# Two 64-column products or one 128-column product for each step that brings coefficients into place

## The chip, the cores and the metric

The kernel runs on one core of a Trainium2 chip. A core has TensorE (matmuls; PE in the profile, its weight loads PEld), VectorE (DVE), ScalarE (ACT), GpSimd (POOL), and queues that start transfers between HBM and the on-chip memory. A matmul holds one operand, the weights (`lhsT`), in its 128 x 128 array and streams the other (`rhs`) past it; the result goes to PSUM. The metric is the time of one launch on the device in microseconds.

## The reference

Two layers of the same kind act on `x` of shape (2, 56, 128, 128): two images, 56 channels, 128 x 128 points. Each layer is a Fourier attention block with a residual around it:

```python
xn = inorm(xa, g1, b1)                      # xa: every channel by itself
k, q, v = (fno_layer(xn, w) for w in (K, Q, V))   # 1 channel -> 8 heads
attn = softmax(q . k / 128, axis=-1)        # 56 x 56, for each head
out = fno_layer(attn . v, P)                # 8 heads -> 1 channel
att = inorm(out + xa)
h = fno_layer(inorm(att), M0, norm=True, act=gelu)
h = fno_layer(h, M1, norm=True)
x = x + inorm(h) + att                      # with group norm on the input
```

`fno_layer` takes the 2-D Fourier transform, multiplies 32 x 16 low modes by complex coefficients (`Kw`, `Qw`, `Vw`, `Pw`, `M0w`, `M1w`), transforms back and adds a 1 x 1 product of the input. All of it is float32.

## The kernel before

The kernel never builds `k`, `q` and `v` in space. It works on the modes: `modes_chain` brings each image's channels into 32 x 16 modes, `gram`, `scores` and `softmax_chain` form the attention, `values`, `mix_chain` and `heads` apply it, `norms_chain` and `h_chain` work out the norms and the two small layers, `gelu` and `end` come back to space in eight pieces an image. The products with coefficients need these as small matrices, so `prepare` (lines 361 to 466), once a layer, multiplies the raw coefficients (`stage`) to the combinations that are needed (`cpt`), brings them into place with `relay`, and spreads them out into `WU`, `WT` and `WM` with `build` and a last loop.

`relay` (lines 468 to 489) is called three times a layer, with n = 16, 16 and 4 coefficient rows. It transposes `cpt` (8 n rows come out), lays the result out in `L` with four VectorE multiplications by a mask (`m8`), so that each of 8 steps t and two halves e has 64 columns, and then has TensorE multiply these by another mask (`m16`, n columns). That is one unit of 16 products: for each t, e = 0 goes to PSUM partitions 0 to 63 and e = 1 to partitions 64 to 127, given by `tile_position`. One copy brings the 8 n columns from PSUM to `tcs` (tile `tc` in the profile), from where `build` and `WM` take them. `L` lies in `WT` for the first call and in `stage` for the others, so in the profile the products are `psum<-C,WT` with 64 weight columns and `psum<-C,stage`.

The order is written out by hand. Each operation, or group of operations in `with work.unit()`, is a unit; the long string `ORDER` says in which order the units are issued and on which engine, and `PLACES` says which banks of PSUM each takes. `Work.issue` (line 209) makes all calls, so nearly every instruction has the line L215. An engine does its instructions in the order in which they were issued, each when the semaphores that it waits for are there. The work of a `relay` stands in TensorE's queue between work of `turned`, `gram`, `modes_chain`, `scores` and, for the second layer, of `h_chain` and `end` of the layer before.

Names in the profile's steps: `mv` are the sums from which `modes_chain` takes mean and variance, a product with `group` (128 columns); `fwg` is the transform's matrix scaled by that; `sq` is a sum in `h_chain`, a product with `fold` (64 columns); `spread` (line 559, `psum<-C,f` there) lays a column of `f` out over partitions; `inverse` (line 522) ends in VectorE transposes into `WT`.

## Time and profile before

| | |
|---|---|
| median of 3 runs | 369.89 us (367.32 to 373.07) |
| profiled execution, its own time | 372.52 us |
| its span, first to last instruction | 370.7 us |
| mean granted TensorE clock | 0.957 |
| busy: TensorE, its weight loads, VectorE, ScalarE, GpSimd | 329.5, 240.7, 266.2, 232.3, 240.8 us |
| matmuls and weight loads | 7362 of each |

A row of the timeline has the start, the duration, the engine, the code line, the operation, the tiles (out <- in), the shapes and the count; in brackets stands the idle time of the engine before it and what ended it. For a matmul the first shape is that of the weights (rows x columns), the second that of what streams. Rows that follow one another in the same group are merged, and a matmul's end is modelled, so what counts on TensorE is when things start. "issue" is idle time that ends with nothing the profile shows. In the chain of waits a row has start, duration and whose work it is. In the table by windows the last three columns are the granted clock of TensorE, the DMA share and GB/s.

### The profile page before, as it was taken

To read this page: it belongs to the slowest core of one execution; us is meant where nothing else is said; L and a number is where in the kernel's file an instruction comes from. 1 tells how busy PE (TensorE), PEld (TensorE's weight loads), DVE (VectorE), ACT (ScalarE), POOL (GpSimd) and SP (SyncE) were. 2 spreads that over 40 slices of the span, in tenths; PEclk is the share of its full clock that TensorE was granted. 3 is DMA by queue.
4 is the path that set the end of the run, shared out by engine and by line. 5 is a ranking of instruction groups with operands and counts; after the bars stand their busy time and mean duration, and the time that the engine had idled before them with its cause. 6 is when DMAs were issued, how large, how long until landed. Compare 5 with 4: busy or idle time off the path is not lost.

```text
span 370.7 us, 16358 instructions
## 1 busy us (share of the span) xinstructions
PE 329.5 (89%) x7362; PEld 240.7 (65%) x7362; DVE 266.2 (72%) x515; ACT 232.3 (63%) x338; POOL 240.8 (65%) x224
## 2 busy tenths in 40 slices
PE   2549989999999999998979999899999999999970
PEld 1445975888776656567866987698676546665540
DVE  4866963546868876787678956456698877989980
ACT  0437954454456978788883986544476878888400
POOL 7540489719987893278579797716965381467970
PEclk9999998999999999898868999999999999999995
DMA  7998223000053535201512076500045454202886
GB/s 211 273 257 247 63 58 107 4 4 5 2 137 71 156 104 137 52 2 54 177 51 71 10 222 188 147 5 4 2 126 135 129 165 103 52 4 78 252 260 206
DMA packets 15973, 40.14 MB, mean 108 GB/s; under 512 B 2560, under 2 KB 2816, under 8 KB 15904
## 3 DMA queue, kind: packets, MB, share of 16 engines
q1 hardware_dynamic: 12692, 30.84, 30.1%
q10 hardware_dynamic: 3212, 8.27, 7.6%
q8 instruction: 57, 0.93, 1.1%
q14 instruction: 12, 0.10, 0.1%
HBM read 24.42 MB, written 14.68 MB: 105 GB/s over the span
## 4 chain that ended last, share of the span: by engine, by line
PE 54%; DVE 18%; POOL 8%; issue 7%; DMA 6%; ACT 4%; DVEq 0%; ACTq 0%; POOLq 0%
PE psum L215 54%; DVE P L215 7%; DMA X<-x 6%; POOL X L215 4%; DVE X L215 3%; DVE WU L215 3%; DVE WT L215 2%; ACT P L215 2%; DVE psum L215 1%; POOL P L215 1%; POOL der L215 1%; DVE f L215 1%; POOL WT L215 1%; POOL WM L215 1%; ACT WU L215 1%
## 5 line engine op out<-in xcount | busy, mean ns | idle before, releaser
L215 POOL TENSOR_TENSOR X<-X,gvr 128x1024 f32<-128x1024 f32 x29 | 68.5, 2372 | 3.8 <-DMA store<-X 3.7
L215 ACT ACTIVATE junk<-P 128x1024 uint8<-128x1024 f32 (+1 forms) x56 | 56.6, 1011 | 2.1 <-DVE X L215 1.3
L215 PE MATMUL psum<-P 128*56 128x56 f32 (+2 forms) x1664 | 56.5, 224 | 0.0
L215 PEld LDWEIGHTS psum<-C,P 32*128 32x128 f32 (+4 forms) x1124 | 41.5, 159 | 22.1 <-ACT P L215 5.4
L215 PEld LDWEIGHTS psum<-P 128*56 128x56 f32 (+1 forms) x1664 | 50.0, 134 | 4.1 <-ACT P L215 1.1
L215 PE MATMUL psum<-C,P 32*128 32x128 f32 (+4 forms) x1124 | 49.5, 253 | 3.1 <-DVE P L215 1.0
L215 ACT COPY P<-psum 128x896 f32<-128x896 f32 (+3 forms) x30 | 26.9, 916 | 24.3 <-PE psum L215 24.2
L215 POOL TENSOR_TENSOR P<-P,X 128x1024 f32<-128x1024 f32 x14 | 32.8, 2370 | 10.7 <-ACT P L215 10.7
L215 ACT ACTIVATE P<-psum,cols 128x1024 f32<-128x1024 f32 x32 | 34.6, 1115 | 7.5 <-PE psum L215 7.2
L215 PE MATMUL psum<-C,X 56*128 56x56 f32 x512 | 26.1, 263 | 13.2 <-DMA C<-const_all 7.0
L215 ACT ACTIVATE P<-psum 128x896 f32<-128x896 f32 (+1 forms) x28 | 23.9, 857 | 20.4 <-PE psum L215 16.2
L215 PE MATMUL psum<-X,BTx 57*64 57x512 f32 x256 | 35.2, 631 | 0.8 <-ACT WT L215 0.7
L215 PEld LDWEIGHTS psum<-C,X 56*128 56x128 f32 x512 | 23.1, 172 | 17.1 <-DMA X<-x 7.3
L215 DVE SCALAR_TENSOR_TENSOR X<-psum,cols,xr 128x1024 f32<-128x1024 f32 x22 | 27.6, 1272 | 7.3 <-ACT xf L215 3.2
L215 ACT ACTIVATE P<-P,shz,gv 128x1792 f32<-128x1792 f32 x14 | 25.6, 1875 | 11.0 <-PE psum L215 10.6
L215 POOL TENSOR_TENSOR X<-P,X 128x1024 f32<-128x1024 f32 x12 | 28.3, 2378 | 3.7 <-DVE P L215 3.7
L215 DVE STREAM_TRANSPOSE P<-psum 128x448 f32<-128x448 f32 (+1 forms) x24 | 23.6, 1012 | 8.9 <-PE psum L215 8.9
L215 DVE COPY P<-psum 128x896 f32<-128x896 f32 (+4 forms) x27 | 20.4, 766 | 12.7 <-PE psum L215 12.4
L215 POOL TENSOR_TENSOR X<-X,xr 128x1024 f32<-128x1024 f32 x9 | 21.3, 2370 | 10.2 <-ACT X L215 10.2
L215 PE MATMUL psum<-C,WT 32*128 32x128 f32 (+1 forms) x544 | 23.4, 295 | 1.8 <-DVE P L215 1.3
L215 PEld LDWEIGHTS psum<-C,WT 32*128 32x128 f32 (+1 forms) x544 | 19.8, 196 | 8.0 <-DVE P L215 4.6
L215 DVE SCALAR_TENSOR_TENSOR P<-P,hs,psum 128x1024 f32<-128x1024 f32 x17 | 21.2, 1269 | 3.5 <-PE psum L215 3.5
(210 smaller groups left out, 649.7 us busy)
## 6 DMA issues: line engine op xcount, KB each, us to landing
xr<-x SPq DMA_DIRECT2D x30, 224.0 KB
store<-X SPq DMA_DIRECT2D x29, 224.0 KB
xr<-store SPq DMA_DIRECT2D x27, 224.0 KB
out<-P SPq DMA_DIRECT2D x23, 224.0 KB
X<-x SPq DMA_DIRECT2D x9, 448.0 KB
X<-x ACTq DMA_DIRECT2D x7, 448.0 KB
out<-P ACTq DMA_DIRECT2D x9, 224.0 KB
xr<-store ACTq DMA_DIRECT2D x5, 224.0 KB
```

The source lines that it names most:

```text
L215: getattr(engines[letter], method)(*args, **kw)
```

## The change

Each `relay` issues 8 products in place of 16. The weights of a step t are all 128 columns (e, c, j, s in one), the output is all 128 partitions, and no `tile_position` is given. What streams is the same, as are the unit's place in `ORDER`, its bank, and the copy behind it.

```diff
         with work.unit():
             for t in range(8):
-                for e in range(2):
-                    T.matmul(
-                        pt[64 * e : 64 * e + 64, n * t : n * t + n], lhsT=L[:rows, t, e].rearrange("p c j s -> p (c j s)"),
-                        rhs=C["m16"][:rows, :n], start=True, stop=True, tile_position=(0, 64 * e), skip_group_check=True,
-                    )
+                T.matmul(
+                    pt[:, n * t : n * t + n], lhsT=L[:rows, t].rearrange("p e c j s -> p (e c j s)"),
+                    rhs=C["m16"][:rows, :n], start=True, stop=True, skip_group_check=True,
+                )
         copy("SV", tcs[:, :, o : o + n], pt[:, : 8 * n].rearrange("p (t n) -> p t n", t=8))
```

## The prediction

> **What bounds the kernel now.** I read the page first, for the engine that the end hangs on, then the chain of waits around the places where the changed products run, then the timeline of TensorE there.

> ```profile
> span 370.7 us, 16358 instructions
> PE 329.5 (89%) x7362; PEld 240.7 (65%) x7362; DVE 266.2 (72%) x515; ACT 232.3 (63%) x338; POOL 240.8 (65%) x224
> PEclk9999998999999999898868999999999999999995
> PE 54%; DVE 18%; POOL 8%; issue 7%; DMA 6%; ACT 4%; DVEq 0%; ACTq 0%; POOLq 0%
> ```

> TensorE holds 54% of the chain that ends last, three times as much as the next engine. The changed edit touches TensorE alone, so the first question is what it does to TensorE's time, and the second which of the places lies on that chain. The six units that change (three calls of `relay` per layer) are these rows of TensorE's timeline, in order of time:

> ```profile
> 41.28 1.06 PE L215 MATMUL psum<-C,WT 128*64 128x16 f32 x32
> 45.09 1.11 PE L215 MATMUL psum<-C,stage 128*64 128x16 f32 x32
> 53.24 1.05 PE L215 MATMUL psum<-C,stage 32*64 32x4 f32 x30
> 183.85 1.89 PE L215 MATMUL psum<-C,stage 128*64 128x16 f32 x32
> 192.12 1.17 PE L215 MATMUL psum<-C,stage 128*64 128x16 f32 x32
> 222.04 1.10 PE L215 MATMUL psum<-C,stage 32*64 32x4 f32 x32
> ```

> I call them U1 to U6. Each has 32 records for 16 products, so one float32 product is two passes, and each pass has its own weight load. (U3 begins with two more records at 53.11, hence x30.) The chain of waits around them:

> ```profile
> 33.93 11.25 PE psum L215 x346
> 45.20 1.02 ACT P L215 x2
> ...
> 50.67 2.26 PE psum L215 x62
> 52.95 0.17 DVE gs L215
> ...
> 187.56 3.17 PE psum L215 x20
> 190.76 3.29 DVE WT L215 x2
> 194.12 37.18 PE psum L215 x958
> ```

> U1 lies inside the stretch from 33.93, U6 inside that from 194.12. U2 and U3 lie between pieces, U4 before 187.56 and U5 beside the 3.29 us of VectorE. These four need their neighbours, below.

> **What a unit costs now and after.** Removed: in each unit 16 of 32 weight loads and 16 of 32 matmuls, 96 of each over the kernel. In their place the 16 loads that are left have 128 columns, not 64. What goes into the products and the copy out of PSUM behind them is the same, so the other engines' work is unchanged.

> ```profile
> L215 PE MATMUL psum<-C,WT 128*64 128x16 f32 x32 | 1.1, 207 | 0.0
> ```

> The view that groups instructions by shape (after the count: busy us, mean ns, idle before) gives 0.21 us for one matmul of U1. So U1's last matmul starts 1.06 - 0.21 = 0.85 us after its first, and U2's, of the same shape, 1.11 - 0.21 = 0.90. Two records, one for each 64-column half, thus come about every 0.90 / 15.5 = 58 ns. After the change one record stands for the two. It is longer or shorter than 58 ns according to what a 128-column load takes. Two operations of this kernel show it, each a product in two passes with next to nothing to stream (2 columns and 1 column), one with 128 columns of weights, one with 64:

> ```profile
> 52.53 0.19 PEld L215 LDWEIGHTS psum<-mv,C 128*128 128x128 f32 x1 [0.33 <-issue]
> 52.64 0.19 PEld L215 LDWEIGHTS psum<-mv,C 128*128 128x128 f32 x1
> 52.53 0.27 PE L215 MATMUL psum<-mv,C 128*128 128x2 f32 x1
> 52.66 0.25 PE L215 MATMUL psum<-mv,C 128*128 128x2 f32 x1
> 179.78 0.13 PEld L215 LDWEIGHTS psum<-sq,C 128*64 128x64 f32 x1
> 179.83 0.14 PEld L215 LDWEIGHTS psum<-sq,C 128*64 128x64 f32 x1
> ```

> From load to load it is 0.11 us with 128 columns and 0.05 with 64. A load goes with its columns. And one 64-column load alone takes 0.05, while the units do two of them in 0.058: the two halves load side by side today, each into its own half of the array's columns. This is the step on which the forecast hangs. The change does not halve the loading, it puts two loads that ran together one behind the other, in one wide load. A unit of 16 wide loads takes 16 x 0.11 = 1.76 us in place of 16 x 0.058 = 0.93, which is **0.83 us more**, at full clock. The bounds of this term: -0.47 (16 x 0.029, if a record needed only half of the 58 ns) and +1.15 (16 x (0.13 - 0.058), the 0.13 from matmul to matmul of the 128-column pair, if its slower start holds for every pass). I take 0.83, the nearest rows' value.

> [...]

> U4 ran at half clock:

> ```profile
> 183.80:185.60 1.80, 1.80 (x36) 1.75 (x32) 1.08 (x6) 1.68 (x4) 1.01 (x3) 0.50 0.02 7
> ```

> The last three columns are the granted clock, 0.50, and the DMA share and rate. Its 1.89 us less one matmul of 0.21 are 1.68, or 0.108 a pair, close to twice U2's. I double the price with it: +1.7 us.

> A second price is not in a load. The unit now uses the array's columns in one piece, its neighbours in two halves.

> ```profile
> 52.84 0.19 PEld L215 LDWEIGHTS psum<-P,C 128*64 128x64 f32 x2
> ```

> After the wide load at 52.64 the next, of 64-column halves, starts 0.20 us later, though 0.11 would have done: about 0.1 us where the width changes. U1 lies between two pieces of work in halves, so it gains two such changes (0.2), U2 one (0.1, it follows transposes with 128 columns); the others stand beside a change already. As bounds I take 0 and twice that.

> [...]

> **Which of it reaches the end.**

> ```profile
> 45.20 0.92 ACT L215 ACTIVATE P<-psum 128x896 f32<-128x896 f32 x1 [0.49 <-PE psum L215]
> 48.23 1.24 PEld L215 LDWEIGHTS psum<-xf,WU 64*64 64x64 f32 x76 [0.25 <-ACT P L215]
> 50.67 1.02 PE L215 MATMUL psum<-xf,WU 64*64 64x56 f32 x52 [1.06 <-issue]
> 54.29 0.32 ACT L215 ACTIVATE fwg<-C,gv 128x32 f32<-128x32 f32 x1 [2.92 <-POOL gv L215]
> 55.82 3.21 PE L215 MATMUL psum<-P,fwg 128*32 128x448 f32 x16
> ```

> U1: ScalarE at 45.20 waits for TensorE, behind it all follows: +0.83 + 0.2 = 1.03. U2: TensorE waits 0.25 at 48.23 for ScalarE, and that much of U2's delay is covered: 0.83 + 0.1 - 0.25 = +0.68. The idle 1.06 at 50.67 has no releaser in the profile. If it is a stop that ends at a fixed time, it takes up 1.06 of the two; I take it as one that moves along, since what the queue does next hangs on how far it is. U3: the weights `fwg` are there at 54.61, but the products with them begin at 55.82, because TensorE is still at its queue: +0.83 passes.

> ```profile
> 185.65 0.20 DVE L215 TENSOR_SCALAR f<-c,r 56x1 f32<-56x1 f32 x1
> 185.68 0.70 PE L215 MATMUL psum<-C,f 56*64 56x56 f32 x8
> 186.49 0.63 DVE L215 TENSOR_TENSOR psum<-WU,psum 128x448 f32<-128x448 f32 x1 [0.28 <-PE psum L215]
> 194.12 0.38 PE L215 MATMUL psum<-mv,C 128*128 128x2 f32 x2 [0.83 <-DVE mv L215]
> 226.06 0.17 DVE L215 TENSOR_REDUCE mv<-tots 128x2 f32<-128x16 f32 x1 [0.89 <-ACT junk L215]
> 227.19 0.38 PE L215 MATMUL psum<-mv,C 128*128 128x2 f32 x2
> ```

> U4: `spread` (the 8 records at 185.68) stands behind it in TensorE's queue, and VectorE waits for `spread` at 186.49, which leads over `inverse` to the VectorE piece at 190.76 of the chain. Half of `spread` waits for the column that VectorE has ready at 185.85 anyway, so about 0.15 of the delay is covered: +1.55. U5: TensorE is idle 0.83 behind it until VectorE is through with 190.76: 0. U6: the sums `mv` are ready at 226.23 and TensorE gets to them at 227.19, so it is TensorE's queue that is late: +0.83.

> The sum is 1.03 + 0.68 + 0.83 + 1.55 + 0 + 0.83 = **4.9 us**. No term is on the other side: the removed instructions are the pairs' other halves, and their time is in the 58 ns. The profiled execution took 372.52 us with its span of 370.7, so it would become 377.4. It was 2.6 above the median of the runs shown, 369.89 (367.32 to 373.07); the sum put on the median gives 369.89 + 4.9 = **374.8**, 1.3% slower.

> **Rivals.**

> *Faster: the instructions were the price.* If the 58 ns are four instructions being issued (two loads, two matmuls), two instructions take 29, and a unit loses 0.47. On the places that count (U1, U2, U3, U6 and U4, U4 at the same 0.47 since issue need not follow the array's clock) that is -2.4: 367.5. It decides below 58 ns for a wide load. For it speaks how much TensorE waits for nothing named:

> ```profile
> PEld psum L215 <- issue: 42.2, 97, 4.6
> ```

> 42.2 us of idle time in 97 waits. Against it speak the load rows (0.11 at 128 columns) and U4: at half clock the same records take twice as long. [...] Chance 0.05.

> *No change: the halves load one after the other already*, so that 2 x 64 columns are 128: 369.9. Also what it would be if a wide product were carried out as two halves. The single 64-column load of 0.05 beside a pair of 0.058 speaks against it. Chance 0.06.

> *Slower by less: the delay is taken up.* The 1.06 us without a releaser eats U1 and U2 but for 0.65, and U4 runs at full clock in most executions (+0.7 in place of 1.55): 0.65 + 0.83 + 0.7 + 0.83 = 3.0, so 372.9. Chance 0.17.

> *Slower by more: the clock.* The granted clock is 0.50 around U4; a unit that falls into such a stretch costs 1.7 in place of 0.83, and one further half-clock stretch, over U2 and U3 where the chain has its idle 1.06, adds 2 x 0.9, and about 1.7 for the work behind it: 374.8 + 3.5 = 378.3. Nothing in the rows shows that loads move the clock either way. Chance 0.10.

> **How the numbers follow.** Forecast 0.62 (374.8, from about 373 to 376.7 with the bounds of its terms), taken up 0.17, clock 0.10, no change 0.06, faster 0.05. The runs shown differ by 5.75 us among themselves, so a median of a few of them can lie a microsecond or two off. The range 371.0 to 378.3 holds the forecast, the case of delay taken up and most of the clock case, and leaves out the other two. 2%, about what a measurement of this kernel can tell from no change, is 7.4 us: slower by over 2% begins at 377.3, which takes most of the clock case and a little of the forecast, 0.15. Faster by over 2% would need 362.5, below all the cases: 0.02. Within 2%: 0.83.

> **What the changed kernel's profile would show.** The groups with 64-column weights from `stage` and `WT` go, and rows of 128x128 (and 32x128) weights with 16 and 4 columns come, 16 records a unit. Right: a unit takes 1.9 us at full clock and its loads come every 0.11. If it takes 1.1 or 0.6, the load step is wrong, and the first or second rival holds. The starts of later work tell the rest: `mv` at 52.53 late by 1.7, `fwg` products at 55.82 late by 2.5, the chain's piece at 194.12 late by 4.1 and `mv` at 227.19 by 4.9; a delay that shrinks from one to the next shows cover that I have not counted. Half-clock stretches that come or go would show in the granted clock of the windows, and their difference is not the units'. What would make it wrong most simply is that a wide load with 16 columns to stream does not behave as one with 2.

## The result and the profile after

| | before | after |
|---|---|---|
| median (lowest to highest) | 370.0 us (367.32 to 373.07) | 384.52 us (381.91 to 384.93) |
| profiled execution, its own time | 372.52 us | 381.91 us |
| its span | 370.7 us | 380.0 us |
| mean granted TensorE clock | 0.957 | 0.955 |

The changed kernel is slower: ratio 1.0399 (95% interval 1.0344 to 1.0453), some 14.5 us where 4.9 were forecast, and above the range (371.0 to 378.3). Ratios, here and below, are of the mean times of the fast executions, without those that ran a per cent or two longer (medians are of all executions). The profiled execution is the fastest of the four after, and shows 9.3 us of it. The page of the changed kernel, the same lines as before:

```profile
span 380.0 us, 16166 instructions
PE 336.8 (89%) x7266; PEld 247.5 (65%) x7266; DVE 266.5 (70%) x515; ACT 232.3 (61%) x338; POOL 240.6 (63%) x224
PE 68%; DVE 16%; DMA 6%; issue 4%; ACT 3%; POOL 1%; DVEq 0%; SPq 0%; ACTq 0%
```

TensorE has 96 matmuls and 96 loads fewer and 7.3 us more busy time, and it holds 68% of the chain, not 54%. Four of the six units in its timeline, and the loads of the second:

```profile
46.21 1.96 PE L215 MATMUL psum<-C,stage 128*128 128x16 f32 x16
46.21 1.86 PEld L215 LDWEIGHTS psum<-C,stage 128*128 128x128 f32 x16
...
54.42 2.50 PE L215 MATMUL psum<-C,stage 32*128 32x4 f32 x16
...
186.91 1.96 PE L215 MATMUL psum<-C,stage 128*128 128x16 f32 x16
...
227.47 1.94 PE L215 MATMUL psum<-C,stage 32*128 32x4 f32 x16
```

16 loads in 1.86 us are 0.116 each. A unit lasts 1.96 where it lasted 1.11: 0.85 more, as forecast. The places that the prediction named for reading the delay:

```profile
53.62 0.38 PE L215 MATMUL psum<-mv,C 128*128 128x2 f32 x2
...
58.74 1.72 PE L215 MATMUL psum<-P,fwg 128*32 128x448 f32 x8
...
197.59 0.38 PE L215 MATMUL psum<-mv,C 128*128 128x2 f32 x2
...
235.04 0.38 PE L215 MATMUL psum<-mv,C 128*128 128x2 f32 x2
```

Against 52.53, 55.82, 194.12 and 227.19 they are 1.09, 2.92, 3.47 and 7.85 us late; forecast were 1.7, 2.5, 4.1 and 4.9. At 197 the loss is still below the forecast. Between 197 and 235 some 4.4 us come on top, where U6 alone should have cost 0.83. Two things lie there. The first, in the chain of waits:

```profile
197.59 23.78 PE psum L215 x656
221.37 1.94 issue
223.31 15.84 PE psum L215 x303
```

TensorE stands still for 1.94 us in the middle of a run of products whose operands are all there. The view of waits has TensorE's idle time that ends with nothing named ("issue": us, times, longest), and the timeline has the five stops:

```profile
PE psum L215 <- issue: 4.4, 5, 1.9
```

```profile
143.45 0.42 PE L215 MATMUL psum<-WU,C 32*64 32x112 f32 x8 [0.92 <-issue]
179.46 0.46 PE L215 MATMUL psum<-WU,C 32*64 32x112 f32 x17 [0.44 <-issue]
223.31 0.57 PE L215 MATMUL psum<-xf,WU 64*64 64x56 f32 x25 [1.94 <-issue]
263.44 0.38 PE L215 MATMUL psum<-xf,WU 64*64 64x56 f32 x10 [0.33 <-issue]
319.31 0.97 PE L215 MATMUL psum<-xf,WM 64*64 64x56 f32 x26 [0.77 <-issue]
```

None of them was in the trace of before, which had two others (1.06 at 50.67, 0.20 at 55.10), 1.3 us in all. The second thing, by windows of TensorE (granted clock third from last), around U6 of after and then of before:

```profile
227.47:229.41 1.94, 1.94 (x22) 1.00 0.78 266
229.70:233.12 3.42, 3.42 (x32) 0.50 0.43 120
```

```profile
222.00:225.40 3.40, 3.40 (x77) 1.00 0.79 251
225.40:228.80 3.40, 3.40 (x151) 1.00 0.49 130
```

Right behind U6 the clock is at half for 3.42 us, which it was not before; there TensorE's work falls back by a further 1.5 us, from 6.3 to 7.8 behind the trace of before.

```profile
q8 instruction: 57, 0.93, 1.1%
...
q8 instruction: 1, 0.02, 5.8%
```

TensorE has 7266 matmuls, as many loads and 57 others in this trace, 256 instructions for each of the 57 packets (the trace of before, with 57 packets too, has 14781, or 259 each). The places repeat with the same number: from stop to stop the changed kernel's trace has 1280, 1792, 2048 and 2304 instructions, the trace of before 256, to one instruction. Counted from the start of TensorE's instructions in the traces, each of the seven stops, of before and after, begins when 193 of a group of 256 have gone; such a place is called a border below. The same count over the traces of all experiments below gives the same place for every stop there too, apart from the first 36 us of the kernels of experiments 3 and 4. Most borders have no stop: one to seven of some 57 have one. The change takes 32 instructions out of the code at each unit, so it moves these borders, by 32 behind U1 up to 192 behind U6, and others fall into dense runs of small products. **Rival:** the loads and the clock account for everything, and the stops are something that the loads cause.

### The profile page after: what moved, and what is told of

Same layout as the page of the kernel before. It is cut to its first block, busy times and chain, and to the rows that moved or that the text cites. A ratio compares the mean times of both kernels' runs of the same rounds, so it can differ in the third digit from the quotient of the medians.

```text
span 380.0 us, 16166 instructions
## 1 busy us (share of the span) xinstructions
PE 336.8 (89%) x7266; PEld 247.5 (65%) x7266; DVE 266.5 (70%) x515; ACT 232.3 (61%) x338; POOL 240.6 (63%) x224
## 4 chain that ended last, share of the span: by engine, by line
PE 68%; DVE 16%; DMA 6%; issue 4%; ACT 3%; POOL 1%; DVEq 0%; SPq 0%; ACTq 0%
PE psum L215 68%; DVE P L215 5%; DMA X<-x 4%; DVE X L215 3%; DVE WU L215 3%; DMA sm<-small 2%; DVE WT L215 2%; DVE psum L215 1%; ACT P L215 1%; DVE f L215 1%; POOL X L215 1%; ACT WT L215 0%; ACT WU L215 0%; ACT L215 0%; DVEq L1202 0%
## 5 line engine op out<-in xcount | busy, mean ns | idle before, releaser
L215 POOL TENSOR_TENSOR X<-X,gvr 128x1024 f32<-128x1024 f32 x29 | 68.4, 2373 | 3.8 <-DMA store<-X 3.6
L215 ACT ACTIVATE junk<-P 128x1024 uint8<-128x1024 f32 (+1 forms) x56 | 56.6, 1010 | 2.2 <-DVE X L215 1.3
L215 PE MATMUL psum<-P 128*56 128x56 f32 (+2 forms) x1664 | 57.2, 224 | 0.0
L215 PEld LDWEIGHTS psum<-C,P 32*128 32x128 f32 (+4 forms) x1124 | 41.7, 161 | 22.3 <-ACT P L215 5.4
L215 PEld LDWEIGHTS psum<-P 128*56 128x56 f32 (+1 forms) x1664 | 50.2, 134 | 4.3 <-ACT P L215 1.1
L215 PE MATMUL psum<-C,P 32*128 32x128 f32 (+4 forms) x1124 | 49.6, 254 | 3.4 <-DVE P L215 1.0
L215 ACT COPY P<-psum 128x896 f32<-128x896 f32 (+3 forms) x30 | 26.8, 915 | 27.4 <-PE psum L215 27.2
L215 POOL TENSOR_TENSOR P<-P,X 128x1024 f32<-128x1024 f32 x14 | 32.8, 2368 | 10.5 <-ACT P L215 10.5
L215 ACT ACTIVATE P<-psum,cols 128x1024 f32<-128x1024 f32 x32 | 34.6, 1113 | 7.5 <-PE psum L215 7.3
L215 ACT ACTIVATE P<-psum 128x896 f32<-128x896 f32 (+1 forms) x28 | 23.9, 857 | 23.5 <-PE psum L215 15.7
L215 PE MATMUL psum<-C,X 56*128 56x56 f32 x512 | 25.3, 260 | 13.2 <-DMA C<-const_all 7.0
L215 PE MATMUL psum<-X,BTx 57*64 57x512 f32 x256 | 33.7, 613 | 0.7 <-ACT WT L215 0.7
L215 ACT ACTIVATE P<-P,shz,gv 128x1792 f32<-128x1792 f32 x14 | 25.6, 1876 | 13.1 <-PE psum L215 12.6
L215 PEld LDWEIGHTS psum<-C,X 56*128 56x128 f32 x512 | 22.6, 170 | 16.8 <-DMA X<-x 7.6
L215 DVE COPY P<-psum 128x896 f32<-128x896 f32 (+4 forms) x27 | 20.5, 765 | 18.5 <-PE psum L215 18.2
L215 DVE SCALAR_TENSOR_TENSOR X<-psum,cols,xr 128x1024 f32<-128x1024 f32 x22 | 27.6, 1271 | 8.1 <-ACT xf L215 4.5
L215 POOL TENSOR_TENSOR X<-P,X 128x1024 f32<-128x1024 f32 x12 | 28.2, 2373 | 3.7 <-DVE P L215 3.7
L215 DVE STREAM_TRANSPOSE P<-psum 128x448 f32<-128x448 f32 (+1 forms) x24 | 23.6, 1011 | 9.4 <-PE psum L215 9.4
L215 POOL TENSOR_TENSOR X<-X,xr 128x1024 f32<-128x1024 f32 x9 | 21.3, 2368 | 10.2 <-ACT X L215 10.2
L215 PEld LDWEIGHTS psum<-C,WT 32*128 32x128 f32 (+1 forms) x528 | 19.7, 194 | 7.7 <-DVE P L215 4.2
L215 PE MATMUL psum<-C,WT 32*128 32x128 f32 (+1 forms) x528 | 23.1, 292 | 1.4 <-DVE P L215 1.2
L215 DVE SCALAR_TENSOR_TENSOR P<-P,hs,psum 128x1024 f32<-128x1024 f32 x17 | 21.3, 1270 | 3.2 <-PE psum L215 3.1
```

The source lines that it names most:

```text
L215: getattr(engines[letter], method)(*args, **kw)
```

## Experiments

All kernels with "idle instructions" have `nop(hint="pad", nofuse=True)` in TensorE's queue, which computes nothing and takes up one instruction of the code: 32 of them move a stop by 32 instructions (experiment 2). What one takes in time is in experiment 4.

**1. The change with the borders of before.** Four idle instructions behind each wide product make up for the two loads and two matmuls of the product that is gone.

```diff
+                T.matmul(pt[:, n * t : n * t + n], ...)      # the wide product of the change
+                for _ in range(4):
+                    T.nop(hint="pad", nofuse=True)
```

> The 8 wide products of each unit stay, and 32 instructions that do nothing stand beside them in TensorE's queue, so that every later instruction has the place in the code that it had in the kernel before. Theory 'code' (the loads cost about 0.8 us a unit, and the rest of the loss is TensorE's code arriving late, at borders of 256 instructions that the removed 32 a unit have moved): the loads' share alone is left, 373 to 377 us, and the stop of 1.9 us at 223.31 is gone. Rival 'loads and clock' (the rest comes from the wide loads or the clock): 382 to 385, no change against the changed kernel.

Measured: 380.0 us (375.99 to 380.74), ratio 1.0223 (1.0155 to 1.029). The stop at 223 is gone; all stops in its trace are:

```profile
PE psum L215 <- issue: 0.5, 2, 0.4
```

It is faster than the changed kernel, but above the 373 to 377 expected: code is a part of the loss, and the rest is more than the price of the loads. Since the two had run on different chips, both ran again on one.

> The changed kernel once more, beside the kernel with wide products and the borders of before, on one chip. It gives the loss that has to be shared out: 3.4 to 4.5% over the kernel before, 382 to 385 us.

> Wide products with 32 idle instructions a unit, borders as before, once more beside the changed kernel. If the code's share is what the first comparison gave, this is 1.2 to 2.4% faster than the changed kernel (4.5 to 9 us) and 1.6 to 2.8% slower than the kernel before. If the first comparison was a difference between two chips, the two are within 1%.

Measured: the changed kernel 1.0418 (1.0352 to 1.0483), the one with the borders of before 1.0293 (1.0237 to 1.035), medians 384.77 and 379.5 beside 370.18. The difference, 1.25% or 4.6 us, is what moving the borders costs (the first pair, on two chips, gives 6.5); by the spread of the executions it is good to some 2.5 us. The stops are not of one size: the changed kernel's second trace has the same five places and two more, and more time at all but one of them. Three of its stops, its total, and the total of the kernel with the borders of before:

```profile
142.75 0.42 PE L215 MATMUL psum<-WU,C 32*64 32x112 f32 x8 [2.73 <-issue]
179.73 0.46 PE L215 MATMUL psum<-WU,C 32*64 32x112 f32 x17 [1.25 <-issue]
225.61 0.57 PE L215 MATMUL psum<-xf,WU 64*64 64x56 f32 x25 [2.23 <-issue]
```

```profile
PE psum L215 <- issue: 8.5, 7, 2.7
```

```profile
PE psum L215 <- issue: 2.3, 3, 0.9
```

These three stops begin at the same instruction (x8, x17, x25 matmuls are left of the group in both executions), and last 0.92 and 2.73, 0.44 and 1.25, 1.94 and 2.23. The place is the code's, the length is that of the execution.

**2. Borders moved, loads of before.** The kernel before, with idle instructions ahead of everything.

```diff
     with tc.manual_schedule():
+        for _ in range(64):          # and 96
+            nc.tensor.nop(hint="pad", nofuse=True)
```

> The kernel before with its 16 products a unit, and 64 instructions that do nothing at the start of TensorE's queue: behind the last unit the code then has the borders of the changed kernel (six times 32 less and 64 more differ by 256). Theory 'code': the time moves by more than 1 us from that alone, with the stops near 263 and 319 (0.3 and 0.9 us) as in the changed kernel; most likely 371 to 374. Rival 'loads and clock': 370, within 1 us.

> The kernel before with 96 instructions that do nothing at the start of TensorE's queue: between the fifth and the sixth unit the code has the borders of the changed kernel. Theory 'code': a stop of about 2 us among the products of xf with WU near 217, and 371 to 375 in all. Rival 'loads and clock': no such stop, 370, within 1 us.

Measured: 377.65 us, ratio 1.0164 (1.0062 to 1.0265), and 380.21 us, 1.0223 (1.014 to 1.0306). By 27 us both are level with before (their first products with `fwg` start at 26.98 and 27.37, those of before at 27.37), so here the idle instructions themselves cost nothing. Both lose more than expected, with not one product changed. With 64, of the two stops expected the one near 263 is there (0.38 us at 258.00, with 10 products left as in the changed kernel), the one near 319 is not. The stop near 217, expected with 96, is there, and with 64 there is one in the same group. The rows are first with 64, then with 96; the third is from the kernel with 128 idle instructions (below).

```profile
219.87 0.34 PE L215 MATMUL psum<-xf,WU 64*64 64x56 f32 x9 [1.06 <-issue]
```

```profile
140.63 1.53 PE L215 MATMUL psum<-xf,WM 64*64 64x56 f32 x24 [2.06 <-issue]
...
220.42 0.57 PE L215 MATMUL psum<-xf,WU 64*64 64x56 f32 x25 [0.83 <-issue]
```

```profile
220.05 0.81 PE L215 MATMUL psum<-xf,WU 64*64 64x56 f32 x41 [2.23 <-issue]
```

Behind the stop 9, 25 and 41 products of the same group are left. Each 32 instructions more (16 loads and 16 matmuls) move the stop by 16 matmuls: it sits at a place of the code. And 25 is what the changed kernel has at 223.31, as its borders between U5 and U6 differ from these by a full 256. The rival, for which these kernels had to stay at 370, falls as the whole account: borders cost time without any wide load. What the clock adds is measured in experiments 6 and 7. The total of the stops is 5.9 us in 7 with 64, and 6.5 in 7 with 96.

**3. The changed kernel moved back at the end.**

```diff
+        for _ in range(192):
+            nc.tensor.nop(hint="pad", nofuse=True)
```

> The changed kernel with 192 instructions that do nothing at the start of TensorE's queue: behind the last unit the code has the borders of the kernel before, ahead of it other ones. Theory 'code': the stops near 263 and 319 go, the time moves by more than 1 us from the changed kernel's, most likely to 377 to 382. Rival 'loads and clock': 383 to 385.

Measured: 386.83 us (383.61 to 394.58), 1.04 (1.0331 to 1.0469). The expected gain didn't come, and the kernel cannot tell why: its first matmul starts at 14.93 instead of 6.96, as 192 idle instructions at the very start take up that time themselves (14.4 us by the 0.075 us each of experiment 4). Of the stops near 263 and 319 its trace has neither, but others at 120, 150, 183 and 227 (0.6 to 1.8 us).

**4. Idle instructions where TensorE waits.** To move the borders without a late start they were put ahead of the first product with `mv`, behind 4.41 us of idle time.

```diff
+        with work.unit():
+            for _ in range(128 if whole else 0):          # and 224
+                T.nop(hint="pad", nofuse=True)
             T.matmul(p[:, :2], lhsT=C["group"], rhs=mv, start=True, stop=True)
```

> The kernel before with 128 idle instructions near 20 us, where TensorE waits 4.4 us for the sums mv, so that they cost no time themselves; behind them all borders of the code lie 128 earlier. Theory 'code': in the trace of before the 256 instructions ahead of a border so placed took 2.27 us at 92, 2.33 at 139, 2.68 at 216, 2.57 at 253 and 2.25 at 307; a block is there about 3 to 4 us after the one ahead of it was entered, so stops of 0.5 to 1.5 us near these places, and 374 to 379 in all. Rival 'loads and clock': 370, within 1 us.

> The kernel before with 224 idle instructions near 20 us, where TensorE waits 4.4 us: all borders behind them lie 32 instructions later in the work than before. In the trace of before no run of 256 instructions ahead of such a border is shorter than 2.8 us, where the borders of before have one of 2.42 and the two stops at 50.67 and 55.10. Theory 'code': few stops, 368 to 371, against 381 with 128 idle instructions at the same place. Rival 'it is the idle instructions, not the place of the borders': slower than with 128, over 381.

Measured: 381.03 us, 1.0272 (1.0185 to 1.0359), with 128; with 224 a median of 382.71 (374.57 to 385.55), without an interval. Both are off the expectation, and the reason is one that I had not reckoned with. The first `mv` product with 128 and with 224:

```profile
27.57 0.56 PE L215 MATMUL psum<-mv,C 128*128 128x2 f32 x2 [8.21 <-issue]
```

```profile
35.59 0.56 PE L215 MATMUL psum<-mv,C 128*128 128x2 f32 x2 [15.44 <-issue]
```

96 more idle instructions take 7.2 us more: 0.075 each where nothing hides them. So in the profiled execution 11.2 of the 13.1 us that the span is longer with 224 are lost by 35.59. That execution is the longest of six (385.55 us); the shortest took 374.57, and no trace tells what it lost there. The median is what the rival named (over 381), but with this start it doesn't speak for it, and the test of that place of the borders failed. Behind the start its trace has few stops, as expected: three, of 1.25, 1.47 and 1.09 us, where 128 has seven. With 128 the start is 3.2 us late, but that is made up by 60 us, where this kernel is 1.5 us ahead of before. What it loses, it loses later, at stops of 2.23 (220.05, above) and 2.12 (287.38) and smaller ones: this one does bear the theory out. The 3 to 4 us that its expectation gives a block were an estimate: in the traces of before and after the seven stops end 2.8 to 4.7 us behind the border ahead of theirs (the one at 55.10 ends 4.43 behind 50.67). (Within the units of experiment 1 the idle instructions are hidden: the 16 wide loads of U2 take 1.86 us with them, in the second run of that kernel, and 1.86 without.)

**5. The two layers apart.** Wide products with the borders of before in one layer, the products of before in the other.

```diff
+                if work.note == "prep0":          # "prep1" for the second layer
+                    ...                           # as in experiment 1
```

> Wide products with 32 idle instructions a unit in the first layer alone (U1, U2, U3); the second layer as in the kernel before, all code borders as before. Theory 'loads as priced': 2.5 us more than before (1.03 + 0.68 + 0.83), 372 to 374. Rival 'loads cost more wherever they are': half of what all six units cost with the same borders (8 to 9 us), 374 to 375.5, spread over the three places. If the extra came from the clock in the second layer, this kernel shows nothing of it.

> The same for the second layer alone (U4, U5, U6). Theory 'loads as priced': 0.83 to 1.55 for U4, nothing for U5, 0.83 for U6, so 1.7 to 2.4 more than before, 372 to 373. Theory 'clock': U4 and U5 lie where the granted clock is 0.50 for 10 to 20 us, the longer loads keep it there, and this kernel has most of the extra: 375 to 378, with a mean clock of 0.95 or less against 0.96 of the kernel before.

Measured: 1.0122 (1.0044 to 1.0199) for the first layer, 1.0102 (1.0048 to 1.0156) for the second, 375.67 and 373.54 us beside 371.64. Together 2.24%, where all six had 2.23 and 2.93% in experiment 1: the places add up as far as the intervals tell. Each is above its forecast (4.5 against 2.5 us, 3.8 against 2.4), though both intervals reach down to it. The second layer alone does not have most of the extra (375 to 378 us), as the theory "clock" had expected of U4 and U5.

**6. The loads doubled.** Each wide product is issued twice, so that a unit has 64 instructions as before, none of them idle.

```diff
+                for _ in range(2):
+                    T.matmul(pt[:, n * t : n * t + n], ...)      # the wide product, the same both times
```

> Each wide product is issued twice, so each unit has 16 products and 64 instructions as before, all with 128-column weights (the second writes the same result again). Borders of the code as before, no idle instructions. Theory 'loads': a unit takes 32 x 0.112 = 3.6 us in place of 0.93, 2.65 more; with U1, U2, U3, U4, U6 uncovered and U5 but for 0.8 covered no longer, 5 x 2.65 + 1.8 = 15, so 384 to 388. Rival 'the idle instructions made the loss of the kernel with the same borders': 370 to 373.

Measured: 397.86 us, 1.0703 (1.0599 to 1.0808), 26 us more, where 15 were worked out for the doubled loads alone. It settles that the loads cost time without any idle instruction. And it shows what comes on top. Three of its units, and the windows of TensorE in which its clock was at half, but for the end of the kernel:

```profile
50.46 3.95 PE L215 MATMUL psum<-C,stage 128*128 128x16 f32 x32
62.83 5.87 PE L215 MATMUL psum<-C,stage 32*128 32x4 f32 x32
...
244.51 3.73 PE L215 MATMUL psum<-C,stage 32*128 32x4 f32 x32
```

```profile
43.62:50.45 6.83, 6.83 (x106) 0.50 0.37 86
53.86:60.69 6.83, 6.83 (x162) 0.50 0.05 11
64.10:74.34 10.24, 10.24 (x115) 0.50 0.36 98
193.81:221.11 27.30, 26.04 (x203) 0.50 0.18 53
248.42:251.83 3.41, 3.41 (x28) 0.50 0.34 75
sum 54.61, PE 53.35; mean PE 10.67
```

Each unit runs into a half-clock stretch, or has one right behind it, all multiples of 3.41 us, although TensorE is busy through nearly all of them. The mean granted clock is 0.92.

**7. More streamed beside the same loads.** In experiment 6 the clock is at half for 54.61 us, and TensorE is busy for 53.35 of them. Whether the few columns streamed beside the loads (16 or 4) have to do with it, no run had shown. So the wide products were made to stream 128 columns. The surplus is overwritten by the next step or never read, and what is used stays the same.

```diff
-                    pt[:, n * t : n * t + n], ..., rhs=C["m16"][:rows, :n], ...
+                    pt[:, n * t : n * t + 128], ..., rhs=Ct[:rows, _PARTS["m16"][0] : _PARTS["m16"][0] + 128], ...      # m16 and what follows it
```

> Each wide product issued twice, each streaming 128 columns in place of 16 (or 4). Theory 'clock': about 15 us over the kernel before, the doubled loads alone, 384 to 388, with a mean clock of 0.95 or more; more work done and over 8 us faster than the same kernel with 16 columns. Rival 'the loads themselves': 395 to 400, mean clock 0.92 again.

Measured: 388.2 us, 1.0537 (1.0471 to 1.0604), clock 0.965 in the profiled execution. The unit and the window behind it:

```profile
47.54 3.84 PE L215 MATMUL psum<-C,stage 128*128 128x128 f32 x32
...
50.40:57.00 6.60, 6.35 (x197) 1.00 0.06 13
```

With eight times the streaming this unit, U2, takes no longer, the half-clock stretch behind it is gone, and the kernel is 1.66% (6.2 us) faster by the ratios, 9.7 by the medians, which are of two chips. Ahead of the end of the kernel the trace has 20.5 us at half clock, where the one of experiment 6 has 54.6. So in these two kernels, with the same loads, 128 columns streamed in place of 16 or 4 leave 34.1 us less at half clock. Not all the stretches go: at U3, U4 and U6 some remain, of 6.83, 3.41 and 3.41 us, the first here, and why is open (U3 and U6 have weights of 32 rows, not 128).

```profile
60.20:67.03 6.83, 6.83 (x92) 0.50 0.48 138
```

> The changed kernel, each of its wide products streaming 128 columns in place of 16 (or 4). Theory 'clock': the mean granted clock rises from 0.95 to 0.965 or more, and the time falls by 2 to 5 us against the changed kernel; the stops of the code stay. Rival 'clock not set by what is streamed': the same time as the changed kernel, or slower.

Measured, beside the changed kernel on one chip: 379.82 us, 1.0278 (1.0218 to 1.0338), against 1.0418. So the clock costs the changed kernel about 1.4%, or 5.2 us. Its trace has 10.2 us at half clock ahead of the end, where the second trace of the changed kernel has 30.7. The stops are still there (4.6 us in 7).

> The kernel with wide products, 32 idle instructions a unit and all code borders as before, but each product streams 128 columns in place of 16 (or 4), the rest being written where the next step overwrites it or nobody reads. [...] Theory 'clock' (a stretch of wide loads with little streamed lets the granted clock fall to half in the 3.4 us behind it, and that is what the loads cost beyond 0.83 a unit): the half-clock stretches behind U2, U3 and U6 go, mean clock 0.957 or more, 374 to 376.5. Rival 'the loads themselves' or 'the clock falls for another reason': as the kernel that streams 16, 379 to 382, or more if the streaming shows.

Measured, with both the borders of before and the streaming: 375.69 us, 1.0199 (1.0154 to 1.0244). This is the change without most of its two side effects (its trace has one stop of 0.3 us, and 10.2 us at half clock ahead of the end): 7.3 us, still 2.4 above the forecast of 4.9. The gain against experiment 1 (1.0223 and 1.0293) is less clear than in the pair before it.

> The kernel before, each of its 64-column products streaming 64 columns in place of 16 (or 4). [...] Theory 'clock': the half-clock stretch behind U3 (55.76 to 59.17 in before) goes, perhaps part of 182 to 199, mean clock above 0.96, 367 to 370. Rival 'clock not set by what is streamed': 370 to 372, the streaming costing up to 0.4 us a unit.

Measured: 369.38 us beside 369.06, 1.002 (0.9985 to 1.0055). For the kernel before, with 64 columns streamed in each of its products, nothing is to be had. Its units cost it no measurable time by the clock. The 0.4 us a unit that its expectation gives the streaming is shown by no run: the whole kernel, with six units, took 0.3 us more by the medians.

**8. One unit of the change alone.** Wide products in U5 only, where the loads are covered, and no idle instruction.

```diff
+                if work.note == "prep1" and o == 16:
+                    T.matmul(pt[:, n * t : n * t + n], ...)      # the wide product of the change
```

> The kernel before with wide products in U5 alone and no idle instruction anywhere: 32 instructions fewer behind 192. U5 has 0.83 us of TensorE's idle time behind it, so its loads cost nothing. Theory 'code': the borders behind it move by 32, to where the kernel with 224 idle instructions had stops of 1.47 and 1.09 near 217 and 222 (on the scale of before): 1 to 3 us slower than before, 370 to 373. Rival 'loads alone': the same as before within 1 us.

Measured: 371.78 us beside 370.18, 1.0067 (1.002 to 1.0114). The time lies where the theory "code" put it. The trace, of the fastest of its executions, has no stop behind U5, so that this loss is the code's is not shown.

No kernel of these is faster than the kernel before.

## Why the prediction was wrong

**A term that was not in the sum.** "No term is on the other side: the removed instructions are the pairs' other halves, and their time is in the 58 ns." This is the step that failed, together with the clock below: two terms were put at nothing. The removed instructions were costed at nothing, when they also set which products stand at the borders, the places, 256 instructions apart, where the traces have their stops. Moving the borders costs 4.6 us in the changed kernel (experiment 1), and alone, with the loads of before, 6 to 8 (experiment 2). The sign was there to be read in the trace of before: 1.06 us of "issue" at 50.67 in a run of products whose operands were there, and 0.20 at 55.10, 256 instructions further.

**The stop at 50.67** was taken "as one that moves along". It did not move, it went: in the changed kernel no stop is left there, and the delay fell from 2.05 us behind U2 to 1.09 at `mv`. The rival "the delay is taken up" was right on this, for this one place, while the five new stops, which nobody looked for, gave more than it took.

**The clock.** "Nothing in the rows shows that loads move the clock either way", and the rival with one more half-clock stretch got 0.10. The doubled loads have 54.6 us at half clock ahead of the end with 16 or 4 columns streamed and 20.5 with 128, the changed kernel 30.7 and 10.2 (experiments 6 and 7); in the changed kernel that difference goes with some 5.2 us. The rival was right that half-clock time is added, but it had no cause for it, and its chance and its size (3.5 us) were too low. The mean clock of the two profiled executions (0.957 and 0.955) hides it. Of the ten timed executions of the changed kernel the clock is 0.929 to 0.955, while after_busy, the version that streams more, has 0.962 to 0.976, and the kernel before on the same chip 0.956 to 0.976. The two shares overlap, as a stop can be followed by half clock (below): on that chip the change costs 4.18%, or 15.5 us, and with the 7.3 of experiment 7 taken off, 8.2 are left for code and clock together, not 4.6 + 5.2 = 9.8.

**The load price** was right for a unit. A wide load takes 0.116 us where 0.11 was read off two rows, and a unit is 0.85 longer where 0.83 was forecast. The rivals "the instructions were the price" and "no change" fall with the same rows. What it comes to over the kernel is not shown as well: the doubled loads with the streaming of experiment 7 lose 5.4% (4.7 to 6.0), 19.8 us, where 15 were worked out. And the lower end of the forecast, 373, does not follow from the bounds given for its terms, as the lower bound of the load price alone leads to the 367.5 of the first rival.

**The covers.** U1 gives 1.1 (1.03 forecast), U5 nothing (nothing), U6 0.84 before the clock falls (0.83). U4 ran at full clock in this execution and gives about 0.4 in place of 1.55; in the second trace it ran at half, 3.60 us long. U3 gives about 1.5 in place of 0.83, as the clock fell to half in its second half (at 55.6).

**What stays open.** Without most of the code's and the clock's share 7.3 us are left (5.7 to 9.0), where 4.9 were forecast. Where the other 2.4 come from is open. The one trace of that kernel does not show it: it has less half-clock time ahead of the end than the trace of before (10.2 us against 23.9) and less time at stops (0.3 against 1.3), and the two profiled executions, 373.62 and 372.52 us, differ by only 1.1. Shares taken on different chips are good to a microsecond or two (the kernel before has medians from 369.06 to 371.64 us on them).

## What to carry to other kernels

Before you add or remove instructions on TensorE, look in its timeline for idle time with no releaser inside a run of products whose operands are there, and count 256 instructions on from it: where such a border fell into a dense run of small products, the stops of these traces were 0.2 to 2.7 us long (one to seven of some 57 borders had one), and any edit ahead of it that changes the number of instructions moves all that follow. To price an edit without this, put the instructions that it removes back as idle ones beside work that hides them. And where loads take the place of streaming, look at the granted clock right behind them, not of the whole run: ahead of the end of the kernel the half-clock stretches last 3.41 us or a multiple of it here, and the mean clock was 0.957 before and 0.955 after.

## What the chip showed that I had not expected

- Stops of TensorE, up to 2.73 us, from 36 us on only at places a multiple of 256 instructions apart, and at one to seven of some 57 of these. Three stops of the changed kernel are at the same instruction in two executions, with lengths of 0.92 and 2.73, 0.44 and 1.25, 1.94 and 2.23 us. The seven of before and after end 1.2 to 1.5 us after a 16 KB packet of the instruction queue; the one of 0.90 us at 48.74 in the second run with the borders of before has no such packet in the 2.7 us ahead of its end.
- The half-clock stretches of experiment 6: a granted clock of 0.50 for 54.61 us, with TensorE busy for 53.35 of them. With 128 columns streamed instead of 16 beside the same loads (experiment 7) the clock behind U2 is 1.00.
- A stop can be followed by half clock as well; that it brings the clock down is not shown by itself. Around the stop at 287.38 of the kernel with 128 idle instructions:

```profile
284.40:287.80 3.40, 1.28 (x42) 1.00 0.66 201
287.80:298.00 10.20, 10.20 (x84) 0.50 0.17 48
```

- An idle instruction took TensorE 0.075 us where nothing hid it (7.2 us for 96 in experiment 4).
